# Chunk 4 of the feed-forward part moved between the value products and the value projection, with four smaller moves, in a one-core attention and feed-forward layer

## The chip, the cores and the metric

The kernel runs on one core of one Trainium2 chip. The metric is the device time of one execution in microseconds (us), the median of three runs. The engines are named as the profile names them: PE (matrix products; PEld is its weight load), DVE (vector), ACT (activations and scalings), POOL (GpSimd) and SP (here it only issues DMAs).

## The reference

8192 tokens (4 x 2048) of width 256 pass through one layer. Every group of 32 consecutive tokens attends only within itself, with a decay mask; then comes a gated feed-forward part of hidden width 768 whose weights are integers of -127 to 127 with one common scale:

```
S   = (x Wq^T)(x Wk^T)^T * mask          (32 x 32 in each group, mask = decay^(i-j), i >= j)
O   = S (x Wv^T)
h   = layernorm(x + (sigmoid(x Wg^T) * O) Wo^T + x)
f   = (silu(h wg^T) * (h wu^T)) wd^T     (weights = integers / 127)
out = layernorm(h + f)
```

All inputs and outputs are float32.

## The kernel before, in words

**Tiling.** The tokens are cut into 16 blocks of 512 (TB), each of four groups of 128 tokens. PE keeps float32 accuracy by splitting numbers. In an attention projection (`three`, L520) both factors are split into parts hi, lo and gap: PE first makes the hi and lo products into two banks, ACT multiplies each bank by WHOLE (L527, "rescale" below), and only then PE adds the gap products (`others`) onto it. There are four such projections: p_g (gate), p_y (queries and keys in one matrix), p_v (values), p_o (output). In the feed-forward part each activation has a hi part in fp32r and a lo part in float16; the integer weights are held in both types. The hidden width is six chunks (hc 0 to 5) of 128. `ffn_up` (L864) makes one chunk: two products of hi and two of lo for fg (gate) and fu (up), s = Silu(fg) on ACT (L884), u = fu*s on DVE (L895), u_hi on ACT (L900), u_lo on POOL (L901). `kinds` (L871) says whether hi or lo comes first: hi in even chunks, lo in odd ones. `held=True` returns the step that makes u, so that the caller can put other work ahead of it. `ffn_down` makes fdn and the second residual r.

**Order.** Nearly every instruction goes through `in_turn`, so each engine runs its instructions in the order in which the code writes them. Four blocks are in work at once. The loop over b (L1093) does the feed-forward part of block b together with the scores, value products and output projection of block n = b + 2 and the projections of block m = b + 3. For b = 0 to 12 ("more") the order on PE from the scores on is: scores ps (L648, fp32, tiles 128x32), value products po (L684, fp32, tiles 64x64), p_v hi and lo, chunk 4 (hi, lo), p_v gap, p_g hi and lo, chunk 5 (lo, hi), p_o hi and lo, p_g gap, p_o gap, fdn. The next block starts with chunks 0 and 1, p_y hi and lo, chunk 2, p_y gap, chunk 3. For b = 13 there are no new projections, and the code has its own branch. The last two blocks come after the loop (L1205 on), with `lagging` set: the splits of u are put off until after the next Silu.

**Small steps.** `scale_and_shift` (L373) turns mean and variance of h into a scale and a shift of 128x4 numbers: reciprocal on DVE, two multiplications and a product on POOL. ACT then normalizes h (L420, four instructions of 128x256). `move_h` transposes h with DVE and SP's DMAs. `look_up` (L290) finds the largest integer of each of nine weight pieces on DVE; `count_wide` counts pieces over 128 with a tiny product pw (L309), which decides at the very end whether a slow path must run. `cast_fd` makes the down weights of both types on ACT in block 0.

**Buffers.** PSUM is one pool of eight banks in rotation (`bank`, L117): a new bank waits until the one taken eight banks earlier has been read. The integer pieces lie in buffers that u_hi takes over later, one after another.

Of the kernel before, what the change touches and what calls it, by code (L numbers as in the profile page):

```python
# [76 lines left out]
def kernel(  # L77
# [292 lines left out]
    def root_in_turn(mv, kind, name):  # L370
        return root(mv, name, kind[0], order=in_turn)

    def scale_and_shift(mv, std, kind, name):  # L373

        on_r, on_dst = kind
        scale, minus, shift = (
            small.tile([P, NG], F32, tag=tag, name=f"{tag}_{name}")
            for tag in ("scale", "minus", "shift")
        )
        in_turn(nc.vector.reciprocal(std, std))  # L380
        for t, sign in ((minus, -1.0), (scale, 1.0)):
            nc.gpsimd.tensor_scalar(t, std, sign * on_dst / on_r, None, ALU.mult)
        nc.gpsimd.tensor_tensor(shift, mv[:, :, 0], minus, ALU.mult)  # L383
        return scale, shift


# [474 lines left out]
        while late_splits:  # L861
            late_splits.pop(0)()

    def ffn_up(b, hT, uT, chunks, cols=slice(0, TB), held=False):  # L864

        n = cols.stop - cols.start
        for hc in chunks:
            pg = bank(f"fg_{b}_{hc}_{cols.start}")[:, :n]
            pu = bank(f"fu_{b}_{hc}_{cols.start}")[:, :n]

            kinds = (0, 1) if hc % 2 == 0 else (1, 0)  # L871
            for kind in kinds:
                for pb, w in ((pg, fg), (pu, fu)):
                    for dc in range(KD):
                        product = nc.tensor.matmul(  # L875
                            pb,
                            lhsT=w[kind][:, dc, hc * P : (hc + 1) * P],
                            rhs=hT[kind][:, dc, cols],
                            start=(kind == kinds[0] and dc == 0),
                            stop=(kind == kinds[1] and dc == KD - 1),  # L880
                        )
                        in_turn(product)
            s = work.tile([P, n], F32, tag="s", name=f"s_{b}_{hc}")
            in_turn(nc.scalar.activation(s, pg, AF.Silu, scale=SCALE / H_UP))  # L884
            no_more_splits()
            if len(uT[0]) == hc:
                for kind, dtype, tiles in zip(("hi", "lo"), (F32R, F16), uT):
                    tiles.append(
                        acts.tile([P, TB], dtype, tag=f"u_{kind}", name=f"u_{kind}_{b}_{hc}")
                    )  # L890

            def multiply(hc=hc, pu=pu, s=s):
                u = work.tile([P, n], F32, tag="u", bufs=3, name=f"u_{b}_{hc}")
                in_steady_turn(
                    nc.vector.scalar_tensor_tensor(u, pu, U_UP / H_UP, s, ALU.mult, ALU.mult)  # L895
                )
                hi, lo = uT[0][hc][:, cols], uT[1][hc][:, cols]

                def split():
                    in_steady_turn(nc.scalar.copy(hi, u))  # L900
                    in_steady_turn(nc.gpsimd.tensor_tensor(lo, u, hi.bitcast(F32), ALU.subtract))  # L901

                if lagging:
                    late_splits.append(split)
                else:
                    split()

            if held:
                return multiply
            multiply()  # L910
# [164 lines left out]
    def up_with_cast(b, hT, uT, hc, kind, pieces):  # L1075

        multiply = ffn_up(b, hT, uT, range(hc, hc + 1), held=True)
        if b == 0:
            cast_fd(kind, pieces)
        multiply()  # L1080
# [12 lines left out]
    for b in range(NB - 2):  # L1093
# [46 lines left out]
        if more:  # L1140
            sT_next = attn_scores(m, yT)
            goT = attn_values(n, sT, v, sg)
            if b == 0:
                look_up(range(4, n_pieces))
            if b == 1:
                count = count_wide()
                n_wide_early = const.tile(
                    [1, 1], I32, tag="n_wide_early", name="n_wide_early"
                )
                nc.vector.tensor_copy(n_wide_early, count)  # L1150
            v_next, v_rest = split_v(m, x_parts)
            go_parts, go_gaps = token_parts(goT, f"go_{n}")
        up_with_cast(b, hT, uT, 4, 1, range(2))
        go_gaps()
        r_before = r_out
        if more:
            v_rest()
            sg_next, g_rest = split_gate(m, x_parts)
            up_with_cast(b, hT, uT, 5, 1, range(2, 3))
            hs[n], out_rest = split_out(n, go_parts)  # L1160
            if b:
                hTs[b + 1] = split_h(b + 1, moving)
            g_rest()
            mv_h = out_rest()
            if b == 0:
                hTs[b + 1] = split_h(b + 1, moving)
            ahead = sT_next, v_next, sg_next
            if m + 1 < NB:
                x_parts, x_gaps = token_parts(xTs[m + 1], f"x_{m + 1}")
            std_h = root_in_turn(mv_h, of_h, f"h_{b}")  # L1170
            if b:
                mv_before, std_before = mv_out, root_in_turn(mv_out, of_out, f"out_{b}")
            back_to_silu()

            def between():
                scales = scale_and_shift(mv_h, std_h, of_h, f"h_{b}")
                if m + 1 < NB:
                    x_gaps()
                return scales

            r_out, mv_out, scales_h = ffn_down(b, uT, hs.pop(b), between)
            if b:
                scales_out = scale_and_shift(mv_before, std_before, of_out, f"out_{b}")
        else:
            multiply = ffn_up(b, hT, uT, range(5, KH), held=True)
            hs[n], out_rest = split_out(n, go_parts)
            multiply()
            hTs[b + 1] = split_h(b + 1, moving)
            scales_out = scales_next
            normalize(r_before, *scales_out)  # L1190
            store(b - 1, r_before)

            def amid():
                return iterated_scale_and_shift(out_rest(), (HALF, 1.0), f"h_{n}")

            r_out, mv_out, scales_h = ffn_down(
                b, uT, hs.pop(b), chunkwise=True, amid=amid
            )
            normalize(hs[n], *scales_h)
            scales_out = iterated_scale_and_shift(mv_out, of_out, f"out_{b + 1}")  # L1200


# [20 lines left out]
        multiply()  # L1223

    lagging = True
    ffn_up(last - 1, hTs[last - 1], uT, range(0, 1))
    up(last - 1, uT, 1, 3)
    for i in range(2):
        groups = range(i * per, (i + 1) * per)
        up_beside(last - 1, uT, 3 + i, r_out, groups)  # L1230
        store_groups(last - 2, r_out, groups)
        if i == 0:
            hTs[last] = transpose_h(last, hs[last], 1)
    up(last - 1, uT, 5, KH)
    up(last, uT_last, 0, 1)
    no_more_splits()
# [322 lines left out]
```

## Time and profile before

| what | value |
|---|---|
| median of three runs | 492.66 us (491.92, 492.66, 492.74) |
| profiled execution, its own time | 491.55 us |
| its span, first to last instruction | 490.0 us |
| outside the span in that execution | 1.55 us |
| granted PE clock over the span | 0.999 |
| PE, share of the span with a product in work | 99% |
| one block of the steady part, po to po | 29.4 to 29.5 us |

The profile is of one execution. It lists busy time by engine, the chain of work that ended last, groups of equal instructions with the mean time of one and the idle time ahead of them, and a timeline in which equal neighbours are merged; a row of the timeline has the start, the time from the first start to the last end, and then the instruction with its count. Products on PE overlap, one starting while another still runs, so for PE it is the distance from one row's start to the next row's start that tells what the row cost.

### The profile page before, as it was taken

What the parts mean: (1) busy time and instruction counts of PE and PEld (TensorE: products, weight loads), DVE (VectorE), ACT (ScalarE), POOL (GpSimd) and SP (SyncE); (2) the same over time, 40 slices, a digit from 0 to 9 for tenths busy, and PEclk for the clock granted to TensorE, in tenths of its full rate; (3) what the DMA queues carried; (4) which work ended last, traced back from release to release, by engine and by line L of the source; (5) the groups of instructions that cost most, each with busy time, mean ns of one, the idle gap of its engine ahead of it and who ended that gap; (6) DMA issues with size and microseconds to landing.
All of it is one profiled execution on the core that took longest, in us unless ns stands there. A gap on an engine that the chain in (4) does not pass through costs nothing.

```text
span 490.0 us, 12290 instructions
## 1 busy us (share of the span) xinstructions
PE 483.4 (99%) x4760; PEld 378.9 (77%) x4760; DVE 330.4 (67%) x756; ACT 372.8 (76%) x699; POOL 292.4 (60%) x324
## 2 busy tenths in 40 slices
PE   9999999999999999999999999999999999999995
PEld 5787786787868878787787868878787787868675
DVE  4576977766775857757676675857757676667556
ACT  4878787687876877788787876878788787785845
POOL 3835656564745657466564755657466564667664
PEclk9999999999999999999999999999999999999999
DMA  8830411311403114131321403123031211103002
GB/s 260 254 91 3 137 44 42 81 46 34 136 23 113 43 46 130 28 104 51 87 80 29 142 22 114 45 56 118 23 109 50 82 45 34 55 19 113 21 25 86
DMA packets 43324, 37.00 MB, mean 76 GB/s; under 512 B 4864, under 2 KB 39168, under 8 KB 43264
## 3 DMA queue, kind: packets, MB, share of 16 engines
q1 hardware_dynamic: 42144, 35.28, 24.3%
q10 hardware_dynamic: 1120, 0.92, 0.6%
q8 instruction: 38, 0.62, 0.5%
q14 instruction: 22, 0.18, 0.1%
HBM read 20.45 MB, written 8.39 MB: 59 GB/s over the span
## 4 chain that ended last, share of the span: by engine, by line
PE 92%; ACT 2%; SPq 2%; POOL 1%; DVE 1%; issue 1%; DMA 0%; DVEq 0%; ACTq 0%
PE fg L875 17%; PE fu L875 16%; PE fdn L730 13%; PE p_v L508 9%; PE p_o L508 8%; PE p_g L486 8%; PE p_y L486 8%; PE po L684 3%; PE fdn L949 2%; PE ps L648 2%; SPq L834 2%; PE fdn L1301 1%; ACT h L420 1%; PE pi L193 1%; PE pv L614 1%; PE pa L763 1%
## 5 line engine op out<-in xcount | busy, mean ns | idle before, releaser
L901 POOL TENSOR_TENSOR u_lo<-u,u_hi 128x512 f16<-128x512 f32 (+1 forms) x98 | 130.0, 1332 | 100.7 <-ACT u_hi L900 94.4
L895 DVE SCALAR_TENSOR_TENSOR u<-fu,s 128x512 f32<-128x512 f32 (+1 forms) x98 | 66.4, 678 | 91.1 <-ACT s L884 76.9
L900 ACT CAST u_hi<-u 128x512 fp32r<-128x512 f32 (+1 forms) x98 | 59.6, 608 | 40.2 <-DVE u L895 40.2
L884 ACT ACTIVATE s<-fg 128x512 f32<-128x512 f32 (+1 forms) x98 | 57.2, 585 | 18.5 <-PE fg L875 18.5
L875 PE MATMUL fg<-hT_hi,fg_hi 128*128 128x512 f32 (+1 forms) x196 | 70.3, 439 | 0.0
L875 PE MATMUL fu<-hT_hi,fu_hi 128*128 128x512 f32 (+1 forms) x196 | 60.5, 390 | 0.0
L875 PE MATMUL fg<-hT_lo,fg_lo 128*128 128x512 f16 (+1 forms) x196 | 58.2, 379 | 0.0
L875 PE MATMUL fu<-hT_lo,fu_lo 128*128 128x512 f16 (+1 forms) x196 | 57.4, 375 | 0.0
L467 POOL TENSOR_TENSOR go_lo<-goT,go_hi 128x512 fp32r<-128x512 f32 x30 | 38.1, 1290 | 25.4 <-ACT go_hi L466 25.4
L467 POOL TENSOR_TENSOR x_lo<-xT,x_hi 128x512 fp32r<-128x512 f32 x30 | 38.4, 1304 | 14.2 <-ACT x_hi L466 14.2
L730 PE MATMUL fdn<-fd_hi,u_hi 128*128 128x256 f32 x312 | 44.6, 285 | 0.0
L473 DVE SCALAR_TENSOR_TENSOR go_gap<-go_hi,goT 128x512 fp32r<-128x512 f32 x30 | 43.4, 1486 | 0.7 <-ACT go_hi L466 0.7
L875 PEld LDWEIGHTS fu<-hT_hi,fu_hi 128*128 128x128 f32 x196 | 36.5, 188 | 8.4
L784 DVE TENSOR_TENSOR h<-p_o,x 128x512 f32<-128x512 f32 x30 | 19.3, 686 | 33.4 <-PE p_o L508 33.4
L875 PEld LDWEIGHTS fg<-hT_hi,fg_hi 128*128 128x128 f32 x196 | 34.7, 189 | 8.9 <-ACT hT_hi L809 0.5
L730 PEld LDWEIGHTS fdn<-fd_hi,u_hi 128*128 128x128 f32 x312 | 38.9, 188 | 0.3
L420 ACT ACTIVATE h<-h,shift_h,scale_h 128x256 f32<-128x256 f32 x52 | 27.0, 590 | 15.3 <-POOL shift_h L383 15.3
L730 PE MATMUL fdn<-fd_lo,u_lo 128*128 128x256 f16 x312 | 38.6, 273 | 0.0
L852 POOL TENSOR_TENSOR hT_lo<-hT,hT_hi 128x512 f16<-128x512 f32 x28 | 35.5, 1292 | 4.0 <-ACT hT_hi L851 3.8
L875 PEld LDWEIGHTS <-fu_lo 128*128 128x128 f16 x196 | 19.2, 98 | 22.1
L527 ACT ACTIVATE p_v<-p_v 128x512 f32<-128x512 f32 x30 | 17.5, 582 | 22.7 <-PE p_v L508 22.7
L875 PEld LDWEIGHTS <-fg_lo 128*128 128x128 f16 x196 | 13.2, 98 | 24.8 <-issue 19.9
(175 smaller groups left out, 1066.4 us busy)
## 6 DMA issues: line engine op xcount, KB each, us to landing
x<-in_x_dram SPq DMA_DIRECT2D x16, 512.0 KB, 3.8
xT<-in_xT_dram SPq DMA_DIRECT2D x15, 512.0 KB, 4.5
hT<-sq SPq DMA_DIRECT2D x224, 32.0 KB, 1.9
out_dram<-r SPq DMA_DIRECT2D x13, 512.0 KB, 3.3
out_dram<-r SPq DMA_DIRECT2D x7, 128.0 KB, 1.7
fg_int<-in_ffn_gT_dram SPq DMA_DIRECT2D x3, 256.0 KB, 7.8
fu_int<-in_ffn_uT_dram SPq DMA_DIRECT2D x3, 256.0 KB, 7.1
fd_int<-in_ffn_dT_dram SPq DMA_DIRECT2D x3, 256.0 KB, 5.9
```

The lines of the kernel that those rows point to most:

```text
L420: nc.scalar.activation(r[:, g, :], r[:, g, :], AF.Identity, bias=shift[:, g : g + 1], scale=scale[:, g : g + 1],)
L467: in_turn(nc.gpsimd.tensor_tensor(lo[:, k, :], t[:, k, :], whole, ALU.subtract))
L473: nc.vector.scalar_tensor_tensor(gap[:, k, :], whole, -WHOLE, t[:, k, :], ALU.mult, ALU.add)
L486: nc.tensor.matmul(pb, lhsT=a[kind][:, k, i * P : (i + 1) * P], rhs=b[kind][:, k, :], start=kind + k == 0, stop=True, skip_group_check=True,)
L508: nc.tensor.matmul(pb[:, j * D : (j + 1) * D], lhsT=b[kind][:, k, g * P : (g + 1) * P], rhs=a[kind][:, k, :], start=kind + k + j == 0, sto ...
L730: product = nc.tensor.matmul(pb[:, j * D : (j + 1) * D], lhsT=part[:, g * P : (g + 1) * P], rhs=w, start=(i == 0), stop=(i == len(terms) - 1),
L852: nc.gpsimd.tensor_tensor(in_order[1], whole, in_order[0].bitcast(F32), ALU.subtract)
L875: product = nc.tensor.matmul(pb, lhsT=w[kind][:, dc, hc * P : (hc + 1) * P], rhs=hT[kind][:, dc, cols], start=(kind == kinds[0] and dc == ...
L884: in_turn(nc.scalar.activation(s, pg, AF.Silu, scale=SCALE / H_UP))
L895: nc.vector.scalar_tensor_tensor(u, pu, U_UP / H_UP, s, ALU.mult, ALU.mult)
L900: in_steady_turn(nc.scalar.copy(hi, u))
L901: in_steady_turn(nc.gpsimd.tensor_tensor(lo, u, hi.bitcast(F32), ALU.subtract))
```

## The change

Six things are changed.

- In the blocks b = 0 to 12 chunk 4 of `ffn_up` now follows the value products directly, with its float16 (lo) products first, by a new argument `low_first`. The splitting of go (`token_parts`) is put between its Silu and its u. p_v and p_g, hi and lo, follow, then p_v gap and chunk 5. The order after chunk 5 stays.
- `scale_and_shift` takes an engine; for h it runs wholly on DVE, in program order. For the second norm ("out") it stays on POOL.
- In block 0, of the look-ups 4 to 8 two stay where they were and three move behind chunk 5; the casts of the down weights are spread over chunk 4, the projections and chunk 5.
- In block 1 the count with its product pw moves from behind the value products to behind chunk 5.
- For the last block the normalization of h moves from ahead of the first Silu of block 14 to behind it.
- In block 14 the transposition of the last h is put ahead of the normalization of r_out and of u of chunk 3.

```diff
-    def scale_and_shift(mv, std, kind, name):
+    def scale_and_shift(mv, std, kind, name, eng=nc.gpsimd, order=free):
...
         for t, sign in ((minus, -1.0), (scale, 1.0)):
-            nc.gpsimd.tensor_scalar(t, std, sign * on_dst / on_r, None, ALU.mult)
-        nc.gpsimd.tensor_tensor(shift, mv[:, :, 0], minus, ALU.mult)
+            order(eng.tensor_scalar(t, std, sign * on_dst / on_r, None, ALU.mult))
+        order(eng.tensor_tensor(shift, mv[:, :, 0], minus, ALU.mult))
...
-    def ffn_up(b, hT, uT, chunks, cols=slice(0, TB), held=False):
+    def ffn_up(b, hT, uT, chunks, cols=slice(0, TB), held=False, low_first=False):
...
-            kinds = (0, 1) if hc % 2 == 0 else (1, 0)
+            kinds = (1, 0) if hc % 2 or low_first else (0, 1)
...
             goT = attn_values(n, sT, v, sg)
             if b == 0:
-                look_up(range(4, n_pieces))
+                look_up(range(4, 6))
+            multiply = ffn_up(b, hT, uT, range(4, 5), held=True, low_first=True)
+            go_parts, go_gaps = token_parts(goT, f"go_{n}")
+            if b == 0:
+                cast_fd(1, range(1))
+            multiply()
+            go_gaps()
+            v_next, v_rest = split_v(m, x_parts)
+            sg_next, g_rest = split_gate(m, x_parts)
+            v_rest()
+            if b == 0:
+                cast_fd(1, range(1, 2))
+            up_with_cast(b, hT, uT, 5, 1, range(2, 3))
+            if b == 0:
+                look_up(range(6, n_pieces))
             if b == 1:
                 count = count_wide()
...
-            v_next, v_rest = split_v(m, x_parts)
-            go_parts, go_gaps = token_parts(goT, f"go_{n}")
-        up_with_cast(b, hT, uT, 4, 1, range(2))
-        go_gaps()
+        else:
+            up_now(b, hT, uT, 4)
+            go_gaps()
         r_before = r_out
         if more:
-            v_rest()
-            sg_next, g_rest = split_gate(m, x_parts)
-            up_with_cast(b, hT, uT, 5, 1, range(2, 3))
             hs[n], out_rest = split_out(n, go_parts)
...
-                scales = scale_and_shift(mv_h, std_h, of_h, f"h_{b}")
+                scales = scale_and_shift(
+                    mv_h, std_h, of_h, f"h_{b}", nc.vector, in_turn
+                )
...
-            normalize(hs[n], *scales_h)
             scales_out = iterated_scale_and_shift(mv_out, of_out, f"out_{b + 1}")
...
     lagging = True
-    ffn_up(last - 1, hTs[last - 1], uT, range(0, 1))
+    up(last - 1, uT, 0, 1)
+    normalize(hs[last], *scales_h)
     up(last - 1, uT, 1, 3)
     for i in range(2):
         groups = range(i * per, (i + 1) * per)
-        up_beside(last - 1, uT, 3 + i, r_out, groups)
-        store_groups(last - 2, r_out, groups)
+        multiply = ffn_up(last - 1, hTs[last - 1], uT, range(3 + i, 4 + i), held=True)
         if i == 0:
             hTs[last] = transpose_h(last, hs[last], 1)
+        normalize(r_out, *scales_out, groups)
+        multiply()
+        store_groups(last - 2, r_out, groups)
     up(last - 1, uT, 5, KH)
```

## The prediction, on record before the changed kernel ran

> **What bounds the kernel now.** I read the busy times first, then the chain that ended last, then PE's timeline in one steady block and at each place where PE lost time.
>
> ```profile
> PE 483.4 (99%) x4760; PEld 378.9 (77%) x4760; DVE 330.4 (67%) x756; ACT 372.8 (76%) x699; POOL 292.4 (60%) x324
> ...
> PE 92%; ACT 2%; SPq 2%; POOL 1%; DVE 1%; issue 1%; DMA 0%; DVEq 0%; ACTq 0%
> ```
>
> PE is the bound, and 92% of the chain. A change pays only where it shortens PE's own sequence or takes away a moment in which PE stands. A busy share of 99% doesn't show such moments, since products overlap; distances between starts do. One steady block (PE, then the weight loads by form):
>
> ```profile
> 205.63 1.16 PE L684 MATMUL po<-sT,v 64*64 64x64 f32 x64
> 206.72 0.72 PE L508 MATMUL p_v<-wv_hi,x_hi 128*128 128x256 f32 x4
> 207.29 0.62 PE L508 MATMUL p_v<-wv_lo,x_lo 128*128 128x256 f32 x4
> 207.74 0.62 PE L508 MATMUL p_v<-wv_hi,x_hi 128*128 128x256 f32 x4
> ...
> L508 PEld LDWEIGHTS p_v<-wv_hi,x_hi 128*128 128x128 f32 x120 | 16.1, 188 | 1.0
> L875 PEld LDWEIGHTS <-fg_lo 128*128 128x128 f16 x196 | 13.2, 98 | 24.8 <-issue 19.9
> ```
>
> The first four p_v products take 0.57 us to the next row, the following four 0.45: the first after po costs 0.11 more. The records of single products say where: the last po starts at 206.577, its neighbours are 7 ns apart, the first p_v and its weight load start only at 206.72, so 0.14 passes before the load begins; the second p_v comes 0.222 after the first instead of 0.113, so 0.109 of the load lies open. A float16 weight load is recorded with 98 ns, an fp32 one with 188. Everything else in a steady block is at its pace: 512-column products are 0.23 apart in fp32r and 0.216 in float16, and a change from float16 to fp32r, which looks like a late second product (0.42), is made up by an early first one (0.03 + 0.42 against 0.22 + 0.23). So in a steady block there is little else to win on PE. Now the places where PE stood:
>
> ```profile
> 68.34 1.09 PE L486 MATMUL p_g<-x_gap,wg_gap 128*128 128x512 f32 x4
> 69.54 1.22 PE L508 MATMUL p_o<-wo_gap,go_gap 128*128 128x256 f32 x8
> ...
> 82.86 0.59 PE L875 MATMUL fu<-hT_lo,fu_lo 128*128 128x512 f16 x2
> 83.42 1.22 PE L486 MATMUL p_y<-x_gap,m_gap 128*128 128x512 f32 x4
> 84.48 0.60 PE L875 MATMUL fg<-hT_lo,fg_lo 128*128 128x512 f16 x2
> ...
> 86.38 0.27 PE L648 MATMUL ps<-yT,xT 128*32 128x32 f32 x8
> 86.91 0.70 PE L648 MATMUL ps<-yT,xT 128*32 128x32 f32 x56 [0.26 <-DVE yT L552]
> 87.53 1.16 PE L684 MATMUL po<-sT,v 64*64 64x64 f32 x64
> ...
> 462.32 0.96 PE L875 MATMUL fg<-hT_hi,fg_hi 128*128 128x512 f32 x2
> 463.12 0.62 PE L875 MATMUL fu<-hT_hi,fu_hi 128*128 128x512 f32 x2
> ```
>
> Block 0, p_g gap and p_o gap: 1.20 + 1.06 to the row that follows, 0.93 + 0.94 in the steady block; 0.39 lost. Block 1: fu lo and p_y gap take 0.56 + 1.06 against 0.24 + 1.12, 0.25 lost, and the scores 1.15 against 0.69, 0.46 lost; 0.71 together. Block 15's first fg pair takes 0.79 against 0.47: 0.33 lost. The causes stand in ACT's and POOL's rows:
>
> ```profile
> 75.61 1.76 POOL L467 TENSOR_TENSOR x_lo<-xT,x_hi 128x512 fp32r<-128x512 f32 x1
> 77.33 0.67 POOL L382 TENSOR_SCALAR minus_h<-rstd_h 128x4 f32<-128x4 f32 x1
> ...
> 78.38 2.08 ACT L420 ACTIVATE h<-h,shift_h,scale_h 128x256 f32<-128x256 f32 x4 [1.87 <-POOL shift_h L383]
> ...
> 461.65 1.07 ACT L809 ACTIVATE hT_hi<-pt 128x512 fp32r<-128x512 f32 x2
> ```
>
> ACT stood 1.87 us for a tiny shift that POOL made behind x_lo; and hT_hi for the last block is ready at 462.73, when PE wants it at 462.33.
>
> **What the Trainium skill says.** "TensorEngine Tiling (Array Packing)", Key Properties: changing the tiling mode drains the engine. The trace agrees: 0.14 us between the last 64x64 product and the next load. "TensorE: Matmul & The Clock Gate", Weight-path perf modes: the fast weight load is on for 128 columns of a type that isn't FP32, measured about twice as fast. The trace agrees: 98 against 188 ns. "SBUF — State Buffer", Who interferes with whom: a DVE instruction with two SBUF inputs contends with a GpSimd one that reads SBUF. The trace agrees: the x_gap beside x_lo in block 1 took 1.77 us, the one before it 0.66.
>
> **The change part by part.** Sums are against the profiled execution (span 490.0, time 491.55); the median of the runs is 1.11 higher, and I carry the same difference over to it.
>
> *Chunk 4's float16 part behind po (13 blocks).* The number of products is the same. The drain stays; the open load becomes a float16 one. Taken from the records it is 188 - 98 = 90 ns shorter: 13 x 0.090 = 1.17 us gained. No row of before has float16 after 64x64 products, so the bounds are 0 (the separate load gains nothing by its speed) and 0.109 (nothing stays open), that is 0 to 1.42. I take 1.17. Against it: in four blocks the p_v products right after po ran 113 ns apart, 118 elsewhere (16 products in 1.92 instead of 1.99 us). Behind fp32r products the p_o ones show 118 in the steady blocks, so I give these up: 4 x 0.066 = 0.26 lost.
>
> What is queued anew: ACT now has s_4, two go_hi and u_hi_4 ahead of the p_v rescale for which p_v gap waits. In the block above chunk 4 ends at about 208.6, p_v at 210.5, p_g at 212.3; PE wants the rescale then. ACT: fg_4 is complete at 208.3, s_4 to 208.9, go_hi to 209.9, u_hi_4 (u_4 on DVE to 209.6, behind goT that ends at 208.37) to 210.5, the rescale to 210.9. Slack 1.4 us; cost nothing. The p_g rescale and the copies of v follow to 213.5, and s_5 isn't due before. The banks of chunk 4 wait for the last p_y copy and fg_2's Silu, both long done; p_v's for fu_2 and fg_3.
>
> *Scale and shift of h on DVE.* Three instructions of 128x4; DVE rows of that size (reciprocal 145 ns, v_h 170) overlap slightly, so 0.5 us of DVE in each of 13 blocks. Behind them wait x_gap, due seven us later, and the second half of the residual. In steady blocks PE isn't waiting, so nothing is gained but small waits of the scores for yT: the scores took 0.69 to 0.75, together 0.17 over 0.69; I take 0.10 gained. In block 1 ACT can start on h at 76.5, after its table load, instead of 78.38. s_0 then ends near 79.1 and u_0, for which DVE is free at 79.7, is made by 80.4 instead of 81.7; the p_y rescale ends near 82.1 and PE wants it at 83.1; yT follows by 85.5, ahead of the scores at 86.1. Both stalls go: 0.71 gained. DVE is then the later of the two; it may start 0.2 later on h's residual because of the moved look-ups, but its x_gap beside x_lo ends with x_lo at any rate. POOL has 1.3 us less.
>
> *Look-ups and casts in block 0.* The stall at 69.5 comes from five look-ups (0.6 us apart) ahead of u_4. Two stay: u_4 is made at 62.0 to 62.7 instead of 63.8 to 64.5, and the p_o rescale ends at 69.3, when PE comes at 69.5. That takes the 0.39 away. But the p_v rescale, now behind u_hi_4 and a cast, ends at about 63.8 with its signal at 63.9, and PE arrives at 63.7: 0.2 lost. Net 0.19 gained, between 0.39 gained and 0.2 lost. The three late look-ups lie in DVE's wait for p_o.
>
> *pw in block 1.* It stood between po and p_v, where the drain was paid anyway, and cost 0.13. Now it stands between fp32r products. By the scores' rows a change into small tiles lengthens the pair before by 0.09, and the load behind is open for 0.11: 0.33 in its place, 0.20 lost; bounds 0 and 0.3.
>
> *Last h.* ACT does s_0 of block 14 while it waited anyway (4.13 us for the term of h), and hT_hi goes ahead of two r_out. hT_hi ends near 460.8 instead of 462.7, PE wants it at 462.3: 0.33 gained. u_3 on DVE moves 1.1 later, to 462.2; its bank is wanted at 462.8. The first store of r_out on SP's queue leaves 0.1 us later, with nothing due behind it.
>
> Sum: -1.17 + 0.26 - 0.10 - 0.71 - 0.19 + 0.20 - 0.33 = -2.04. Profiled 489.5, median 490.6.
>
> **The rivals.** *The float16 load is no help* (it starts after the drain as a separate instruction and its speed is eaten): the 1.17 falls away, 491.8. For it: the separate loads show "issue" as their wait. Against it: float16 follows fp32r with only 10 ns lost. *The drain is hidden too*, if the separate load may go ahead of it: 13 x 0.141 = 1.83 more, 488.8. *The rescale of p_v becomes the bound* (slower): it stands behind four ACT instructions, one of which needs DVE. From 1.4 us of delay on, PE stands in all 13 blocks; 0.3 over that is 13 x 0.3 = 3.9, 494.5. For it: block 0 already comes to that point; against it: DVE is done with goT before s_4 in the block above. *Nothing much*: new small stalls eat the gain, 492.3.
>
> **How the numbers follow.** Forecast 0.55, no help 0.20, hidden drain 0.08, rescale 0.10, nothing 0.07. A measurement of this kernel tells about 0.2% (1 us) from no change. Faster by more: forecast, hidden drain and two fifths of "no help", 0.70 rounded; within: 0.20; slower 0.10. Range: the best ends (1.42, 0.71, 0.33, 0.39, 0.17, no loss) give 3.0, 489.6; "no help" with block 0 at its bad end 492.1; a tenth for the spread of runs at the low end. Left out: 0.18.
>
> **What would show it.** PE's first float16 products behind po some 0.09 us closer than p_v's were; a po-to-po distance near 29.35; no wait in p_y gap and scores of block 1 nor in the first fg of block 15; about 0.2 ahead of p_v gap in block 0. It is wrong if p_v gap waits for its rescale in steady blocks, or if po-to-po doesn't move.

## The result, and the profile after

| | kernel before | changed kernel |
|---|---|---|
| median (runs) | 491.97 us (8) | 490.27 us (8) |
| ratio, 95% interval | | 0.9964, 0.9953 to 0.9975 |
| profiled execution, its own time | 491.55 us | 490.36 us |
| its span | 490.0 us | 488.6 us |

The first three of the eight runs of before are those whose median, 492.66, stands in the table above. The forecast was 490.6, the fall 2.04 us. The medians fell by 1.70, with an interval from 1.23 to 2.31; the spans of the two profiled executions by only 1.4. Two things blur these numbers. One is the start of the kernel (below). The other lies outside the span, where no engine's row shows it: the time of an execution less its span was 1.69 to 2.15 us in the eight runs of the changed kernel (median 1.95), and 1.50 to 1.69 in the 27 runs of before that were made beside hi_first (median 1.57). The median span of these runs fell by 2.05, from 490.50 to 488.45; some 0.4 us of that doesn't arrive in the median of the times. The time outside the span was 1.53 to 1.58 in the six runs of chunk4_only and 1.64 to 2.26 in the 22 of hi_first; what sets it stays open. So small differences are read from the stages, not from the medians.

The page of the changed kernel, busy times and chain:

```profile
PE 482.2 (99%) x4760; PEld 382.1 (78%) x4760; DVE 338.1 (69%) x795; ACT 374.7 (77%) x699; POOL 281.2 (58%) x285
...
PE 98%; DVE 1%; ACT 0%; issue 0%; DVEq 0%
```

DVE has 39 instructions more and POOL 39 fewer, three in each of 13 blocks. The chain shows what the busy share hid: PE is now 98% of it instead of 92%, SP's queue and POOL are gone from it, and ACT all but.

**Where the time went.** I cut both traces at the same products of PE (first scores, po, first p_o, first fdn of each block) and subtracted stage by stage. The first stage, where nothing was changed, is 0.90 longer in the execution after. PE's timeline of before at the start, then that of after:

```profile
1.00 3.81 PE L193 MATMUL pi<-const-float32-0.0 128*128 128x512 f32 x6 [1.00 <-PEq L1544]
4.64 3.60 PE L572 MATMUL pg<-xT,wg 128*128 128x512 f32 x8
8.08 1.89 PE L614 MATMUL pv<-wv,xT 128*128 128x256 f32 x8
```

```profile
1.00 4.18 PE L193 MATMUL pi<-const-float32-0.0 128*128 128x512 f32 x6 [1.00 <-PEq L1558]
4.97 4.16 PE L572 MATMUL pg<-xT,wg 128*128 128x512 f32 x8
8.97 1.89 PE L614 MATMUL pv<-wv,xT 128*128 128x256 f32 x8
```

The first 512-column products are 0.853 us apart, later ones 0.430; in after pg's first two are still 0.854 and 0.570 apart, and the two small products ahead of them 0.21 instead of 0.11. From pv on both run alike. The first scores came between 20.52 and 21.91 us in the traces of this study, 20.54 and 21.41 in two kernels that are the same up to there (cast_late and after), so this is a matter of the execution. The Trainium skill has it too: "TensorE: Matmul & The Clock Gate", What's actually happening, says that the slow first stretch ends with a free-running window and so differs from run to run. It gives ±500 ns for that point; a loss of 0.90 at half pace means that the stretch lasted some 1.8 us longer here (an estimate), so the measured difference is larger. Counted from the first scores to the end, before takes 469.50 us and after 467.21: 2.29 less, and that is what the terms of the prediction have to explain.

| stage | predicted | measured |
|---|---|---|
| float16 part behind po, with the pace of p_v, 13 blocks | -0.91 | -1.26 |
| block 0, stalls of p_o gap and p_v gap | -0.19 | +0.01 |
| block 1, p_y gap and scores | -0.71 | -0.72 |
| pw in block 1 | +0.20 | +0.20 |
| small waits of the other scores | -0.10 | -0.17 |
| last h | -0.33 | -0.32 |
| sum | -2.04 | -2.26 |

Block 0's share of the first row is taken as 0.12, as in the other blocks (in together, where its wait is gone, po to p_o is 9.376 there too). The last 0.03 is what is left of other stages, the largest of them +0.07 and -0.09 ahead of block 0 and -0.05 ahead of the scores of block 2.

The steady block, PE's timeline of after, then the weight loads:

```profile
205.29 1.16 PE L684 MATMUL po<-sT,v 64*64 64x64 f32 x64
206.39 0.60 PE L875 MATMUL fg<-hT_lo,fg_lo 128*128 128x512 f16 x2
206.83 0.59 PE L875 MATMUL fu<-hT_lo,fu_lo 128*128 128x512 f16 x2
207.07 0.82 PE L875 MATMUL fg<-hT_hi,fg_hi 128*128 128x512 f32 x2
207.73 0.63 PE L875 MATMUL fu<-hT_hi,fu_hi 128*128 128x512 f32 x2
208.20 0.63 PE L508 MATMUL p_v<-wv_hi,x_hi 128*128 128x256 f32 x4
...
206.38 0.11 PEld L875 LDWEIGHTS <-fg_lo 128*128 128x128 f16 x2
```

The step from the last po to the first float16 product is 0.151 (0.148 before): the drain is still there. The two fg products then take 226 + 216 ns, what a change into float16 costs everywhere in this kernel, so nothing of the load shows any more. The row of the loads (PEld) tells why: the first two float16 loads take 0.11 together, the second starts 15 ns after the first. In seven blocks po to p_o fell from 9.497 to 9.376, and in the four where p_v had kept a pace of 113 ns by 0.04 to 0.06.

Block 1 and the end, PE's timeline of after:

```profile
83.90 1.28 PE L486 MATMUL p_y<-x_gap,m_gap 128*128 128x512 f32 x4
85.02 0.60 PE L875 MATMUL fg<-hT_lo,fg_lo 128*128 128x512 f16 x2
...
86.92 0.76 PE L648 MATMUL ps<-yT,xT 128*32 128x32 f32 x64
87.61 1.16 PE L684 MATMUL po<-sT,v 64*64 64x64 f32 x64
...
461.25 0.63 PE L875 MATMUL fg<-hT_hi,fg_hi 128*128 128x512 f32 x2
461.72 0.63 PE L875 MATMUL fu<-hT_hi,fu_hi 128*128 128x512 f32 x2
```

p_y gap takes 1.12 to the next row, the scores 0.69, block 15's first fg 0.47: all three stalls are gone. But the way there in block 1 isn't the predicted one (POOL, DVE and ACT of after):

```profile
74.81 2.51 POOL L467 TENSOR_TENSOR x_lo<-xT,x_hi 128x512 fp32r<-128x512 f32 x2
...
76.49 0.86 DVE L382 TENSOR_SCALAR minus_h<-rstd_h 128x4 f32<-128x4 f32 x1
77.27 0.16 DVE L382 TENSOR_SCALAR scale_h<-rstd_h 128x4 f32<-128x4 f32 x1
77.39 0.17 DVE L383 TENSOR_TENSOR shift_h<-mv_a,minus_h 128x4 f32<-128x4 f32 x1
...
77.59 2.08 ACT L420 ACTIVATE h<-h,shift_h,scale_h 128x256 f32<-128x256 f32 x4 [0.65 <-DVE shift_h L383]
```

One instruction of 128x4 took 0.86 us instead of 0.16: it came to its end only when POOL's x_lo did, at 77.32. The Trainium skill, "SBUF — State Buffer", Who interferes with whom, names tensor_scalar among the DVE operations that can use the port pair shared with GpSimd, if their operands suit that mode, and says that whoever comes second then blocks fully. The trace agrees, 0.86 against 0.16. So h starts 6.19 us after the first fdn; the prediction's 76.5 is 5.90 after it on the clock of before, where h started at 7.79. That it isn't later still has two other causes: hT_hi started 0.37 earlier, and the second x_lo took 1.28 instead of 1.76: in before DVE's x_gap had begun just ahead of it (75.56 against 75.61), now x_gap comes behind the small instructions. x_lo ended 5.93 after the first fdn instead of 6.76.

In block 0 a new wait stands ahead of p_v gap (ACT, DVE and PE of after):

```profile
62.89 0.60 ACT L282 CAST fd_lo<-fd_int 128x512 f16<-128x512 int32 x1
63.62 0.62 ACT L900 CAST u_hi<-u 128x512 fp32r<-128x512 f32 x1
64.15 1.06 ACT L527 ACTIVATE p_v<-p_v 128x512 f32<-128x512 f32 x2
...
61.72 1.27 DVE L293 TENSOR_REDUCE top<-fu_int 128x1 f32<-128x512 int32 x2
62.91 0.68 DVE L895 SCALAR_TENSOR_TENSOR u<-fu,s 128x512 f32<-128x512 f32 x1
...
64.78 1.22 PE L508 MATMUL p_v<-wv_gap,x_gap 128*128 128x256 f32 x8
```

PE could have started the gap at 64.51; with the second half of the wait, inside the eight products, 0.40 is lost.

### The profile page after: what moved, and what is told of

Same layout as the page of the kernel before. It is cut to its first block, busy times and chain, and to the rows that moved or that the text cites. A ratio compares the mean times of both kernels' runs of the same rounds, so it can differ in the third digit from the quotient of the medians.

```text
span 488.6 us, 12295 instructions
## 1 busy us (share of the span) xinstructions
PE 482.2 (99%) x4760; PEld 382.1 (78%) x4760; DVE 338.1 (69%) x795; ACT 374.7 (77%) x699; POOL 281.2 (58%) x285
## 4 chain that ended last, share of the span: by engine, by line
PE 98%; DVE 1%; ACT 0%; issue 0%; DVEq 0%
PE fg L875 18%; PE fu L875 18%; PE fdn L730 14%; PE p_o L508 9%; PE p_y L486 9%; PE p_v L508 8%; PE p_g L486 8%; PE po L684 4%; PE ps L648 2%; PE fdn L949 2%; PE fdn L1315 1%; PE pi L193 1%; PE pg L572 1%; PE pv L614 1%; PE pa L763 1%; PE py L593 1%
## 5 line engine op out<-in xcount | busy, mean ns | idle before, releaser
L875 PE MATMUL fg<-hT_hi,fg_hi 128*128 128x512 f32 (+1 forms) x196 | 72.4, 451 | 0.0
L467 POOL TENSOR_TENSOR go_lo<-goT,go_hi 128x512 fp32r<-128x512 f32 x30 | 44.0, 1489 | 18.5 <-ACT go_hi L466 18.5
L473 DVE SCALAR_TENSOR_TENSOR go_gap<-go_hi,goT 128x512 fp32r<-128x512 f32 x30 | 48.4, 1650 | 0.7 <-ACT go_hi L466 0.7
L875 PEld LDWEIGHTS fg<-hT_hi,fg_hi 128*128 128x128 f32 x196 | 35.7, 189 | 10.3
L730 PEld LDWEIGHTS <-u_lo 128*128 128x128 f16 x312 | 28.4, 98 | 3.9
L382 POOL TENSOR_SCALAR minus_out<-rstd_out 128x4 f32<-128x4 f32 x12 | 2.7, 221 | 44.3 <-DVE rstd_out L380 44.3
```

The costliest lines, as they stand in the source:

```text
L467: in_turn(nc.gpsimd.tensor_tensor(lo[:, k, :], t[:, k, :], whole, ALU.subtract))
L473: nc.vector.scalar_tensor_tensor(gap[:, k, :], whole, -WHOLE, t[:, k, :], ALU.mult, ALU.add)
L730: product = nc.tensor.matmul(pb[:, j * D : (j + 1) * D], lhsT=part[:, g * P : (g + 1) * P], rhs=w, start=(i == 0), stop=(i == len(terms) - 1),
L875: product = nc.tensor.matmul(pb, lhsT=w[kind][:, dc, hc * P : (hc + 1) * P], rhs=hT[kind][:, dc, cols], start=(kind == kinds[0] and dc == ...
```

## The experiments

The stages are those above. Theory A is the prediction's: each part works where it stands, by its own mechanism. "From the first scores" is the span without the start.

**Is it the float16 load? (hi_first)** The changed kernel with the fp32r part of chunk 4 first:

```diff
-            multiply = ffn_up(b, hT, uT, range(4, 5), held=True, low_first=True)
+            multiply = ffn_up(b, hT, uT, range(4, 5), held=True)
```

> The changed kernel with chunk 4 still right behind the value products, but hi (fp32r) first. Theory A (what pays is that a float16 weight load isn't left open behind the drain): the open load comes back, now in front of fg_hi: the first product behind po starts its neighbour 0.334 us later, as in block 13, instead of 0.226; po to the first p_o product grows from 9.38 to about 9.49 in every block of the loop, 13 x 0.11 = 1.4 us in all, and the time goes back to about 0.3 us under the kernel before. Rival B (what pays is that p_v no longer stands behind po): the 9.38 stays and the time stays 1.7 us under the kernel before.

Measured: median 491.63 us, ratio to before 0.9989 (0.9982 to 0.9996); from the first scores 468.42, 1.21 more than after. PE's timeline, then the weight loads:

```profile
205.79 1.16 PE L684 MATMUL po<-sT,v 64*64 64x64 f32 x64
206.88 0.73 PE L875 MATMUL fg<-hT_hi,fg_hi 128*128 128x512 f32 x2
207.45 0.63 PE L875 MATMUL fu<-hT_hi,fu_hi 128*128 128x512 f32 x2
...
206.88 0.30 PEld L875 LDWEIGHTS fg<-hT_hi,fg_hi 128*128 128x128 f32 x2
```

The pair behind po takes 0.57 where a pair takes 0.47; by the single records its first product takes 333 ns instead of 226 (float16) or 236 (usual). Po to p_o is 9.472 to 9.476 in blocks 2 to 12, and 0.10 over after in all of blocks 1 to 12; block 0 doesn't change, as its p_v gap waits for the rescale anyway, and that is why 1.21 came back and not the 1.4 expected. Moving p_v away by itself gives 0.02 (9.497 to 9.476); the rest is the type of the first products behind the small tiles. The second fp32 load starts 109 ns after the first, the float16 one 15 ns: this points to the weights, but the experiment changes the type of weights and activations together and doesn't separate them.

**Chunk 4's move alone (chunk4_only)** The kernel before with nothing but this move, in blocks 1 to 12:

```diff
+            if b == 0:
...
+            else:
+                multiply = ffn_up(b, hT, uT, range(4, 5), held=True, low_first=True)
+                go_parts, go_gaps = token_parts(goT, f"go_{n}")
+                multiply()
+                go_gaps()
+                v_next, v_rest = split_v(m, x_parts)
```

with p_g's first products ahead of `v_rest()`; block 0 keeps its order.

> The kernel before with one part of the change alone: in blocks 1 to 12 the float16 part of chunk 4 stands behind the value products, and the p_g products before the gap products of v, as in the changed kernel; block 0, the look-ups, pw, h's scale and shift on GpSimd and the last h stay as before. Theory A (the parts add up; the move is worth 0.12 us a block where p_v kept its pace, 0.05 in the four blocks where it had run at 113 ns): po to the first p_o near 9.38 us in blocks 2 to 12, sum over the twelve blocks 1.0 to 1.2 us less; the stalls of block 1 (0.26 and 0.46) and of block 15 (0.33) and the 0.39 of block 0 are still there; median 490.9, 1.1 below the kernel before, ratio 0.9978. Rival B (the move only pays together with the earlier yT, because the later rescale of p_v and copies of v would hold up what follows): less than half of that, 491.5 or more, with a new wait in p_v gap, p_o or the scores.

Measured: median 490.45 us (6 runs), ratio 0.9963 (0.9951 to 0.9976); from the first scores 467.91, 1.59 less than before. The stages of the twelve blocks give -0.117 to -0.124 in eight and -0.035 to -0.060 in four, sum -1.14, as A had it. The other 0.4 wasn't expected: block 1's stalls are down to 0.03 in p_y gap and 0.31 in the scores, with scale and shift still on POOL. What differs there is the hT of block 1: hT_hi starts on ACT 0.25 us after the first fdn, in the trace of before 0.60. So the size of that stall seems to be partly a matter of when the transfers land (below). The median lies only 0.18 above that of after, which gains 0.70 more from the first scores on; 0.39 of this is the time outside the span, 1.56 here.

**Scale and shift back on POOL (shift_pool)**

```diff
                 scales = scale_and_shift(
-                    mv_h, std_h, of_h, f"h_{b}", nc.vector, in_turn
+                    mv_h, std_h, of_h, f"h_{b}"
                 )
```

> The changed kernel with h's scale and shift back on POOL. Theory A: ACT waits again for a shift that POOL makes behind x_lo, and block 1 loses what it won: the stretch from the first fdn to the scores of block 1 takes 15.79 instead of 15.53 us and the scores 1.15 instead of 0.69, together 0.7; the scores of five later blocks lose up to 0.17 together. Rival B (the earlier go and the moved look-ups had already made room in block 1): both stay as in the changed kernel, within 0.1.

Measured: 491.07 us (one run); from the first scores 467.86, 0.66 more than after. PE, POOL and ACT of this kernel:

```profile
87.16 0.27 PE L648 MATMUL ps<-yT,xT 128*32 128x32 f32 x8
87.69 0.70 PE L648 MATMUL ps<-yT,xT 128*32 128x32 f32 x56 [0.26 <-DVE yT L552]
...
77.70 0.67 POOL L382 TENSOR_SCALAR minus_h<-rstd_h 128x4 f32<-128x4 f32 x1
78.34 0.63 POOL L382 TENSOR_SCALAR scale_h<-rstd_h 128x4 f32<-128x4 f32 x1
78.94 0.20 POOL L383 TENSOR_TENSOR shift_h<-mv_a,minus_h 128x4 f32<-128x4 f32 x1
...
79.17 2.08 ACT L420 ACTIVATE h<-h,shift_h,scale_h 128x256 f32<-128x256 f32 x4 [1.82 <-POOL shift_h L383]
```

The scores of block 1 wait 0.46 again, p_y gap only 0.05 more; four later scores wait 0.05 to 0.08 each, 0.25 together. The cause is as predicted: POOL's three steps behind x_lo are 1.5 us, while on DVE h starts within 0.3 of the end of x_lo. The p_y part of 0.26 didn't come back; h started 7.58 after the first fdn here and 7.79 in before. Against these losses stand two gains of 0.07: in blocks 5 and 11 the p_v products ran 113 ns apart instead of 118, though they stand behind fp32r products as in after.

**pw back behind po (pw_back)** In block 1 the count stands directly behind `attn_values` again.

> The changed kernel with the count's product pw right behind po of block 1 again, ahead of chunk 4. Theory A (pw costs a change of tiling in and out wherever it stands among large products, and behind po that is paid anyway): block 1 from po to the first fdn takes 13.25 instead of 13.44 us, 0.2 less. Rival B (what pw costs is its own time, or the float16 load is opened by it): no less than 13.35.

Measured: 490.11 us (one run). Po to p_o -0.095 and p_o to fdn -0.102, together -0.197: A. But the scores of block 1 took 0.82 instead of 0.69. They stand ahead of pw on PE, so pw can't hold them: DVE's shift_h took 1.20 us beside x_lo in this execution, and hT_hi started 1.17 us after the first fdn, waiting for a DMA.

**Which instruction holds the rescale of p_v in block 0? (lookups, cast_late)** lookups puts all of look-ups 4 to 8 ahead of the first transposition of h; cast_late leaves them and moves the cast:

```diff
             go_parts, go_gaps = token_parts(goT, f"go_{n}")
-            if b == 0:
-                cast_fd(1, range(1))
             multiply()
...
             v_rest()
             if b == 0:
-                cast_fd(1, range(1, 2))
+                cast_fd(1, range(2))
```

> The changed kernel with look-ups 4 to 8 all moved into the idle 3 us of DVE ahead of the first transposition of h, so that none stands ahead of u_4 in block 0. Theory A (the 0.40 us wait of p_v gap in block 0 is a chain of two look-ups on DVE and of one cast on ACT ahead of u_hi_4): u_4 is made 1.2 us earlier, but the cast still holds ACT, so the rescale of p_v comes 0.2 earlier and the wait shrinks from 0.40 to about 0.2. Rival B (look-ups alone): the wait goes to zero. Rival C (go_hi, which waits for goT, sets it): it stays 0.40.

> The changed kernel with the first cast of fd in block 0 moved on ScalarE from between go_hi and u_hi_4 to behind the copies of v. In the changed kernel PE waits 0.40 us there for the rescale of p_v; the cast ends at 63.5, the product u_4 on VectorE, behind two look-ups, at 63.6, u_hi_4 starts at 63.62. Theory A (u_4, and so the look-ups, ends last): the wait ahead of the p_v gap stays at 0.40 within 0.05. Rival B (the cast ends last): the wait falls by 0.3 to 0.4. A loss elsewhere isn't expected: with one cast more behind v, the Silu s_5 is about 0.3 later and the rescale of p_o still on time.

lookups, 489.97 us (one run): none of the three came, the wait did not shrink, it grew by 0.08. u_4 was early, 61.17 to 61.85, but with the look-ups done DVE took the small `wide` into the moments of h:

```profile
48.80 0.66 DVE L305 TENSOR_SCALAR wide<-top 128x9 f32<-128x9 f32 x1
...
61.17 0.68 DVE L895 SCALAR_TENSOR_TENSOR u<-fu,s 128x512 f32<-128x512 f32 x1
```

That delayed the chain h, sq, goT by some 0.3; go_hi ended at 62.45, the cast at 62.95, and u_hi_4 had to wait for the cast. So with u_4 out of the way the chain through goT, go_hi and the cast is next, nearest to C. cast_late, 490.4 us (one run): the wait ahead of p_v gap is the same to 0.03, so A: in the changed kernel u_4 behind its two look-ups ends last. Its expectation failed in one point, a loss elsewhere, in PE's p_o gap:

```profile
68.65 1.09 PE L486 MATMUL p_g<-x_gap,wg_gap 128*128 128x512 f32 x4
69.82 1.22 PE L508 MATMUL p_o<-wo_gap,go_gap 128*128 128x256 f32 x8
70.88 0.87 PE L730 MATMUL fdn<-fd_hi,u_hi 128*128 128x256 f32 x6
```

p_g gap takes 1.17 to the next row and p_o gap 1.06 (0.93 and 0.94 without a wait): 0.36 lost, because a cast more behind v puts s_5, u_hi_5 and the rescale of p_o later. Neither place is free; both waits have the same queue, ACT's.

**How much slack has the rescale of p_v in the steady blocks? (ladder)** Copies of no use between go_hi and u_hi_4, more of them block by block:

```diff
             go_parts, go_gaps = token_parts(goT, f"go_{n}")
+            for i in range(max(0, b - 2) // 2):
+                spare = const.tile([P, TB], F16, tag="spare", name=f"spare_{b}_{i}")
+                in_turn(nc.scalar.copy(spare, goT[:, 0, :]))
```

> The changed kernel with extra work put on ScalarE on purpose, in blocks 4 to 12 only: between the two go_hi and the cast of u_hi_4, one copy of 128x512 (about 0.5 us) more for every two blocks: none in blocks 2 and 3, one in 4 and 5, two in 6 and 7, three in 8 and 9, four in 10 and 11, five in 12. The rescale of p_v comes that much later. It tests the rival 'the rescale of p_v becomes the bound'. Theory A (slack 1.24 us, as the changed kernel's trace has it, the rescale ending at 210.63 and the first gap product starting at 211.92): po to the first p_o stays 9.38 us with none, one and two copies, and grows to about 9.65 with three, 10.15 with four and 10.65 with five, nearly 0.5 per copy. Rival (the real slack is smaller, since half of the rescale or a bank is needed earlier): it grows from the first or second copy. Third possibility: even five copies cost nothing there, and the loss shows up elsewhere, in p_o gap or in the scores. Start of the kernel aside, the whole is about 1.0 + 1.5 + 1.2 us longer in the blocks with three to five copies, span near 492.

ACT and PE in block 8, with three copies:

```profile
298.21 1.91 ACT L1149 CAST spare<-goT 128x512 f16<-128x512 f32 x3
300.02 0.62 ACT L900 CAST u_hi<-u 128x512 fp32r<-128x512 f32 x1
300.55 1.06 ACT L527 ACTIVATE p_v<-p_v 128x512 f32<-128x512 f32 x2
...
301.18 1.10 PE L508 MATMUL p_v<-wv_gap,x_gap 128*128 128x256 f32 x7 [0.41 <-ACT p_v L527]
```

Measured: 497.01 us (one run); from the first scores 6.23 more than after, where 3.7 had been expected. Po to p_o against after: +0.00 with no and one copy, +0.05 and +0.05 with two, +0.69 with three (both blocks), +1.33 and +1.35 with four, +1.99 with five. A copy costs 0.65, not the 0.5 that I had put down; a straight line through these reaches zero at 1.25 us of delay. The slack is Theory A's 1.24; what A had wrong is the length of a copy, so that the cost begins with two copies (1.30 us) and not with three. The rival that the rescale becomes the bound is real, and the changed kernel stands 1.25 us from it in the steady blocks.

**Last h (norm_first, late_transpose)** One of its two moves undone at a time: the normalization ahead of the Silu, or the transposition behind r_out and u_3.

> The changed kernel with one part undone: the normalization of the last h stands again ahead of block 14's first Silu on ScalarE. The changed kernel has hT_hi of the last block ready 1.5 us before PE wants it (459.7 against 461.25). Theory A (each of the two moves alone is enough): hT_hi comes about 0.5 us later, 460.2, and block 15's first fg stays at 0.47 us; nothing lost. Rival B (the Silu's place is what removed the wait): 0.32 us come back there.

> The changed kernel with the other part undone: the transposition of the last h stands again behind the normalization of the first half of r_out and behind the product u_3. Theory A (each of the two moves alone is enough): hT_hi comes 1.0 us later, 460.7, still 0.5 before PE wants it, and nothing is lost in block 15's first fg (0.47 us). Rival B (this move is what removed the wait): 0.32 us come back there.

490.99 and 489.79 us (one run each); from the first scores 467.22 and 467.24, after 467.21. hT_hi ended at 460.84 where PE wanted it at 461.42, and at 460.10 where PE wanted it at 460.64; the first fg took 0.47 in both. A: either move alone is enough, and the second buys only reserve.

**What the runs point to (together)** In block 0 look-ups 4 and 5 go into DVE's wait ahead of the first hT_lo and the first cast into ACT's wait ahead of go_hi; pw goes behind po; chunk 2 of block 13 gets `low_first`:

```diff
-        multiply = ffn_up(b, hT, uT, range(2, 3), held=True)
+        multiply = ffn_up(b, hT, uT, range(2, 3), held=True, low_first=not more)
...
+    look_up(range(4, 6))
     gate = g_rest(hold=True)
...
             goT = attn_values(n, sT, v, sg)
-            if b == 0:
-                look_up(range(4, 6))
+            if b == 1:
+                count = count_wide()
...
-            go_parts, go_gaps = token_parts(goT, f"go_{n}")
             if b == 0:
                 cast_fd(1, range(1))
+            go_parts, go_gaps = token_parts(goT, f"go_{n}")
```

> The changed kernel with what the other runs point to: in block 0 look-ups 4 and 5 stand in VectorE's wait ahead of the first hT_lo (3.3 us idle there), so that u_4 follows goT at once; the first cast of fd goes to ScalarE's wait ahead of go_hi (0.67 us idle), not behind the copies of v, where it cost 0.36 in p_o gap; look-ups 6 to 8 stay where the change put them; in block 1 pw stands right behind po again; in block 13 too chunk 4's neighbour behind po, chunk 2, starts with its float16 part. Theory A: block 0's wait ahead of p_v gap goes (po to p_o 0.28 less, and no new wait of p_o gap), pw costs 0.20 less, block 13 0.10 less; about 0.6 below the changed kernel, median 489.7, ratio to before 0.9953. Rival B: each gain turns into a wait elsewhere (in block 0 the rescale of p_o comes too late for p_o gap; in block 1 VectorE's small steps meet GpSimd's x_lo and the scores wait for yT by 0.1 to 0.5): 490.2 or more.

Measured: median 489.86 us (5 runs), ratio 0.9946 (0.9933 to 0.9960). Block 0 -0.40, with no new wait; pw -0.19; block 13 -0.09, as A. But in the profiled execution block 1 stalled again, 0.33 ahead of the scores and 0.46 in them, so that it took 467.35 from the first scores, 0.14 more than after: by the stages rival B. Of the median's 0.41 under after 0.29 lies outside the span (1.66 against 1.95). ACT, then PE:

```profile
72.84 1.15 ACT L851 CAST hT_hi<-hT 128x512 fp32r<-128x512 f32 x2 [1.78 <-DMA hT<-sq]
...
86.93 0.27 PE L648 MATMUL ps<-yT,xT 128*32 128x32 f32 x8
87.46 0.70 PE L648 MATMUL ps<-yT,xT 128*32 128x32 f32 x56 [0.26 <-DVE yT L552]
```

ACT stood 1.78 us for the transfers that turn h; x_hi, x_lo, the roots and h stand behind hT_hi. In every trace up to here x_lo ends 5.7 to 6.2 us after hT_hi starts, and h starts within 0.3 of that end where scale and shift are on DVE. The start of hT_hi, counted from the first fdn, against the length of block 1's scores, for the changed kernel and its variants with scale and shift on DVE:

| kernel | hT_hi starts | scores |
|---|---|---|
| after, norm_first, late_transpose | 0.23, 0.35, 0.39 | 0.69 |
| lookups, cast_late, hi_first | 0.46, 0.64, 0.85 | 0.69 |
| ladder | 0.43 | 0.78 |
| pw_back | 1.17 | 0.82 |
| together, and once more | 1.77, 1.63 | 1.16, 1.17 |

**Is it the landing of hT, or the program? (together_again, x_before_h)** The same kernel once more, and one in which x is split ahead of the turned h at the end of block 0:

```diff
-            if b == 0:
-                hTs[b + 1] = split_h(b + 1, moving)
             ahead = sT_next, v_next, sg_next
             if m + 1 < NB:
                 x_parts, x_gaps = token_parts(xTs[m + 1], f"x_{m + 1}")
+            if b == 0:
+                hTs[b + 1] = split_h(b + 1, moving)
```

> The kernel 'together' once more, one other execution of the same program. Theory A (the issue of sixteen transfers on SyncE's queue takes 11.5 to 12.7 us from one execution to another, and the scores' wait follows it): with hT_hi starting x us after the first fdn, the scores of block 1 take 0.69 if x is under 1.0, and 0.69 + (x - 1.2) or so above; the start of hT_hi is not at 1.77 again. Rival B (it belongs to the program, through pw's place): hT_hi at about 1.8 and the scores 1.15 again.

> The kernel 'together' with one thing more, at the end of block 0: the parts of x (x_hi on ScalarE, x_lo on GpSimd) stand ahead of the split of the transposed h. Over the traces so far, h's normalization in block 1 starts within 0.3 us of the end of x_lo, and x_lo ends 5.7 us after hT_hi starts, which waits for the last of the sixteen transfers of hT; hT_hi started 0.2 to 0.9 us after the first fdn where the scores of block 1 had no wait, at 1.17 with 0.13 of wait, at 1.77 with 0.46 ('together'). Theory A (the landing of hT sets block 1): x_lo no longer waits for hT, it ends about 5.6 us after the first fdn, h starts there within 0.3, and the scores of block 1 take 0.69 again, 0.46 less than in 'together', whatever the landing; median about 0.4 below 'together', 489.4, ratio to before 0.994. Rival B (pw's place is what brought the wait back): the scores still take 0.8 to 1.15. A loss could come in the float16 part of block 1's first chunk, if hT_lo, now behind x_lo on GpSimd, ends after 6.4 us.

together_again, 490.52 us (one run): hT_hi at 1.63, 0.11 lost ahead of the scores and the scores at 1.17, which is B's outcome. Two parts make up the late start. Counted from the first scores of the kernel, SyncE (SP) begins to issue at the same time in together and in after (37.25 and 37.22), but the first fdn comes at 49.61 instead of 49.98, as block 0's wait is gone; so 0.4 belongs to the program: what was won in block 0 brings block 1 nearer to its transfers. The rest is the issuing: the sixteen issues took 12.69 us in together and 12.55 in together_again, against 11.55 in after. They took 11.5 to 11.8 in eight traces in all, 12.0 to 12.5 in four, with steps of 0.64 but for two or three of 0.8 to 2.0. x_before_h: median 489.34 us (5 runs), ratio 0.9945 (0.9932 to 0.9959), from the first scores 466.62. Its PE, POOL and ACT (in the first row, block 0's p_v gap has no wait):

```profile
63.67 1.10 PE L508 MATMUL p_v<-wv_gap,x_gap 128*128 128x256 f32 x8
...
85.69 0.85 PE L648 MATMUL ps<-yT,xT 128*32 128x32 f32 x64
86.47 1.16 PE L684 MATMUL po<-sT,v 64*64 64x64 f32 x64
...
70.75 2.54 POOL L467 TENSOR_TENSOR x_lo<-xT,x_hi 128x512 fp32r<-128x512 f32 x2 [1.19 <-ACT x_hi L466]
...
76.01 2.08 ACT L420 ACTIVATE h<-h,shift_h,scale_h 128x256 f32<-128x256 f32 x4 [0.67 <-DVE shift_h L383]
```

h starts 5.85 after the first fdn, earlier than in any other kernel, and the scores take 0.78: the stall is gone but for 0.09, with pw still behind po, so pw's place isn't its cause. But in this execution the sixteen issues took 11.6 us and hT came early, so that the run doesn't show that the new order withstands a late landing. The program is that of together until the issues are made, so their length differs from one execution to another; why it is 11.5 or 12.5 us stays open. So do the 0.09 in the scores, as in the ladder: yT was ready 0.4 before in both. Of all kernels this one has the lowest median, 0.93 below after's against another set of runs; the intervals of the two ratios overlap, 0.32 of the 0.93 lies outside the span, and the stages, 0.59 less from the first scores, are the better evidence.

## Why the prediction was right, point by point

- *The level, 490.6*: near by luck in part. It was built on 492.66, 0.69 above the median of eight runs; the fall of 2.04 from 491.97 would have been 489.9. The time outside the span was carried over as constant and grew by some 0.4, and the gain from the first scores on was 2.29, not 2.04. Among the terms, too small a gain behind po and too large a one in block 0 made up for each other in part. (The slow end of the range comes to 492.2 by its own terms, not 492.1.)
- *Float16 load behind po*: right in mechanism (hi_first), too small in size. I took the difference of the two durations, 90 ns; by hi_first the type is worth 100, near the upper end of 109, nothing left open, and moving p_v away another 20: 0.121 per block where the pace stayed. The Trainium skill's "TensorEngine Tiling (Array Packing)", Key Properties, which gives the drain, is borne out on both sides of the change, 0.148 and 0.151.
- *Pace of p_v*: right for this execution, not in its reason. All p_v steps are 117 to 118 ns now, and the four blocks gained 0.04 to 0.06 (0.31 less than the others, 0.26 predicted). But standing behind fp32r products doesn't rule out the faster pace: shift_pool has 113 ns in two blocks. And the p_v of the stage ahead of block 0 ran at 118 in together and at 113 in together_again, one and the same program.
- *Rescale of p_v in steady blocks*: right, slack 1.4 predicted, 1.25 by the ladder.
- *Block 1*: the sum was right, 0.71 against 0.72, the step "ACT can start on h at 76.5" wrong in its reason: h came 0.3 us later, counted from the first fdn, and would have come 1.1 later than predicted had x_lo ended where it did in before. I had written that DVE's x_gap beside x_lo ends with x_lo, and didn't ask the same of the three small instructions put ahead of it. There was enough to spare, h at 6.2 us after the first fdn instead of 7.8, for both stalls to go. And part of the 0.71 seems to have belonged to the execution: in shift_pool POOL's scale and shift cost 0.51 in block 1, and in chunk4_only the stalls of block 1 were 0.34 with scale and shift still on POOL.
- *Block 0*: the gain of 0.39 was right, the new wait was 0.40, not 0.2, so that the net gain of 0.19 didn't come. The term was mis-sized, not its cause: the end that I had put at 63.8 (64.7 in after's times, which are 0.9 later there) is that of the rescale's first half, and PE waits 0.28 for it instead of 0.2; the second half holds PE another 0.12 inside the gap, and that I had left out.
- *pw*, *last h*, *small waits*: right, 0.20, 0.32 and 0.17 (predicted 0.20, 0.33, 0.10). That either half of the last h's move is enough I had not seen.
- *Rivals*: "float16 load is no help" and "drain hidden too" are both refuted by the rows behind po; "rescale becomes the bound" comes true in block 0, and in the steady blocks only in the ladder, from two copies on; "new small stalls eat the gain" comes true in block 0 alone.

## What to carry to other kernels

Behind a run of small-tile products, try products in float16: here the drain of 0.15 us stayed, but the 0.10 of open load behind it went. When small instructions are moved from GpSimd to VectorE to be earlier, look at what GpSimd does at that moment; beside a tensor_tensor of 1.28 us they ended when it ended. A wait that is cured brings everything behind it forward, except what other queues set: in together the 0.40 won in block 0 made block 1 wait for its transfers. And when a wait is cured, ask for the next in line by delaying it on purpose in steps, as in the ladder: the point from which it costs says how much reserve the cure has.

## What was not expected of the hardware

- A DVE instruction of 128x4 took 0.16 us alone and 0.23 to 1.32 when it was caught beside POOL's x_lo; which of the three was caught (minus_h, scale_h or shift_h) changed from one execution to the next.
- The stretch at half pace at the start of PE differed by up to 1.4 us between executions (first scores at 20.52 to 21.91 us), nearly as much as the change is worth. The time outside the span differed too, from 1.50 to 2.26 us.
- Sixteen equal transfers of 32 KB took SyncE 11.5 to 12.7 us to issue, and all of the difference lay in two or three of the steps.
- fp32r products of 256 columns ran at 113 or at 118 ns apart; p_v was at 113 in four blocks of the kernel before, right behind the small tiles, at 118 in all blocks after, and at 113 again in two blocks of shift_pool behind fp32r products. What decides it stays open.
